# Inverse roots of the norms on GpSimd: a power and one Newton step instead of a square root and a reciprocal

## The chip, the cores and the metric

The kernel runs on one core of a Trainium2 chip. Five engines work side by side, each through its own queue and strictly in the order of that queue: TensorE (PE, with its weight loads PEld) for matrix products and transposes, VectorE (DVE), ScalarE (ACT) for functions that it reads from a loaded table, GpSimd (POOL), and SyncE (SP), which here only issues DMAs. They wait for each other through semaphores.

The metric is the time of one execution on the device in microseconds (us), as the median of several runs. Beside it stands one profiled execution, with its own time and a record of its instructions.

## The reference, cut to what matters

Input x has 8 sequences of 512 tokens with 256 features. There are two layers, and each has an attention-like part and an MLP-like part that both read the normalised x:

```python
def _layernorm(x, axis=-1, eps=1e-05):
    m = jnp.mean(x, axis=axis, keepdims=True)
    v = jnp.var(x, axis=axis, keepdims=True)
    return (x - m) / jnp.sqrt(v + eps)
...
xn = _layernorm(x)
x = x + attention(xn) + fp4_mlp(xn)      # layer 0
xn = _layernorm(x)
x = x + convolution(xn) + int4_linear(xn)  # layer 1
```

- The attention of layer 0 has 16 heads of 64 and 64 memory keys, mixes the heads before and after the softmax, and keeps for each row the 64 largest scores.
- The MLP of layer 0 quantises its inputs and its weights to FP4 in blocks of 16.
- The convolution of layer 1 is a gated input, a decaying recurrence along the sequence, and then a second norm over the features, `(y - mu) * rsqrt(var + 0.001)`, before a gated MLP and an output product.

So there are three norms for each sequence: of x (used by attention and by the MLP of layer 0), of the sum after layer 0, and inside the convolution. Each needs an inverse square root for each token, 512 in a sequence. They lie as a tile of 128 partitions by 4 columns.

## The kernel before, in words

**Stages.** A short start loads weights and transposes them (lines 745 to 844). Then comes attention over 8 batches (one sequence each), with 8 groups of rows for each batch (lines 1511 to 1718). A group computes scores on TensorE, evicts them with ScalarE (lines 1016 and 1052), finds the 64th largest value of each row by a search, and applies the result. The search counts values above a threshold on ScalarE (line 1082, Sign with an accumulated sum) or on VectorE (lines 1086 and 1088), and moves the threshold by a secant step (`narrow`, line 1100), which runs on GpSimd or on VectorE. On GpSimd the division in that step is a power with the exponent minus 1 (line 1134, `by<-gap,minus`). The new threshold is the tile `cur`. After the search VectorE picks the survivors (lines 1152, 1155 and 1179), and GpSimd builds the tile `mixd` for the second mixing of heads (line 1271).

A check of the results follows, with a branch that is skipped here. The second stage (from line 1769) holds the MLP of layer 0 for batches 1 to 7 and layer 1 for all batches. Batch 0's MLP and the quantised x of batch 1 are already made at the end of attention (`early_mlp`, line 1425, and `begin_last`, line 1498).

**What sets the order.** Nothing is issued in program order in the two big stages. `Plan` (line 113) collects operations with an engine, a cost and a due time, and `Plan.run` (line 146) simulates the engines and issues, among the operations whose inputs are ready, the one that is due first. In attention the costs are written at each `pl.add`, and the due times come from `DUE` (line 78). In the start and in the second stage `Straight` (line 197) gives the costs (line 232): a DVE operation on few columns 0.17, an ACT operation 0.22 plus 0.83 ns a column plus 1.3 for Sqrt, a POOL operation 0.35 plus 1.8 ns a column. The due time is there the length of the chain that follows (`tails`, line 131). An operation that moves to another engine, or gets another cost, can therefore change the order around it. In the second stage every instruction carries line 276, where `Straight` issues it, so its rows are told apart by the names of their tiles.

**The norms.** There are 32 of them, and each computes mean and variance on VectorE, the square root on ScalarE, the reciprocal on VectorE, and then scales.

- Start, for batch 0: lines 797 to 810, tiles `mv`, `sd` and `scr`.
- Attention, for batches 1 to 7, for `early_mlp` and for `begin_last`: `normed` (line 852) plans four operations, the load on SP (cost 4.0), `stats` on DVE (2.8), `root` on ACT (2.9) and `scale` on DVE (2.0). The tiles are `ln_mv`, `ln_sd`, `ln_ri`, and `scr`.
- Second stage, norm of x for batches 2 to 7 (`quantised`, line 1816) and first norm of layer 1 for all batches (`norm1`, line 1873): `layernorm` (line 347). It makes `ln_mr`, the product of mean and inverse root, on VectorE, and scales on ScalarE.
- Second stage, second norm of layer 1 (`norm2`, line 1892): the variance comes from TensorE in the tile `ps_tr`, `sd` and `ri` hold root and inverse, and TensorE spreads `ri` over the partitions (line 1917).

**POOL's other work.** In the second stage GpSimd does three products of each FP4 quantisation (`fp4_steps`, lines 379, 390 and 391; tiles `q_v` and `q_lo`), the residual sums (lines 1833 and 1837) and the sum with the bias (line 1931).

One more square root, in the first guesses of the search (line 583), is computed once.

Of the kernel before, what the change touches and what calls it, by code (L numbers as in the profile page):

```python
# [8 lines left out]
F32 = mybir.dt.float32  # L9
U32 = mybir.dt.uint32  # L10
AF = mybir.ActivationFunctionType
ALU = mybir.AluOpType
# [3 lines left out]
P = 128  # L16
B, N, D = 8, 512, 256
NT = N // P
# [302 lines left out]
def norm_stats(nc, pool, x):  # L321

    st = pool.tile([P, NT, 6], F32, name="ln_st")
    mv = pool.tile([P, NT, 2], F32, name="ln_mv")
    for t in range(NT):
        nc.vector.bn_stats(st[:, t, :], x[:, t, :])
        nc.vector.bn_aggr(mv[:, t, :], st[:, t, :])
    nc.vector.tensor_scalar(mv[:, :, 1], mv[:, :, 1], 1e-5, None, ALU.add)
    return mv


def norm_root(nc, pool, mv):
    sd = pool.tile([P, NT], F32, name="ln_sd")
    nc.scalar.activation(sd, mv[:, :, 1], AF.Sqrt)
    return sd


def norm_scale(nc, pool, x, xn, mv, sd):
    ri = pool.tile([P, NT], F32, name="ln_ri")
    nc.vector.reciprocal(ri, sd)  # L340
    for t in range(NT):
        nc.vector.tensor_scalar(
            xn[:, t, :], x[:, t, :], mv[:, t, 0:1], ri[:, t : t + 1], ALU.subtract, ALU.mult
        )


def layernorm(nc, pool, x, xn):

    mv = norm_stats(nc, pool, x)
    sd = norm_root(nc, pool, mv)  # L350
    ri = pool.tile([P, NT], F32, name="ln_ri")
    nc.vector.reciprocal(ri, sd)
    mr = pool.tile([P, NT], F32, name="ln_mr")
    nc.vector.scalar_tensor_tensor(mr, mv[:, :, 0], -1.0, ri, ALU.mult, ALU.mult)
    for t in range(NT):
        nc.scalar.activation(
            xn[:, t, :], x[:, t, :], AF.Identity, bias=mr[:, t : t + 1], scale=ri[:, t : t + 1]
        )
# [36 lines left out]
def fp4(nc, pool, src, parts, n, tag):  # L395

    q = {"src": src}
    for k, w in (("amax", n // BLK), ("scale", n // BLK), ("rec", n // BLK), ("v", n), ("a", n), ("lo", n), ("hi", n)):
        q[k] = pool.tile([P, w], F32, name=f"q_{k}_{tag}")[:parts]
    for _, _, step in fp4_steps(nc, q, parts, n):  # L400
        step()
    return q["lo"]
# [241 lines left out]
def block_kernel(ctx: ExitStack, tc: tile.TileContext, a: dict, out: bass.AP):  # L644
    nc = tc.nc
# [3 lines left out]
    const = ctx.enter_context(tc.tile_pool(name="const", bufs=1))  # L649
    ident = const.tile([P, P], F32, name="ident")  # L650
    make_identity(nc, ident)

    dram = ctx.enter_context(tc.tile_pool(name="dram", bufs=1, space=bass.MemoryType.DRAM))
    att = dram.tile([B * NT, P, D], F32, name="att")
# [42 lines left out]
    with ExitStack() as c0:  # L697
# [35 lines left out]
        small = c0.enter_context(tc.tile_pool(name="small", bufs=2))  # L733
        st = c0.enter_context(tc.tile_pool(name="st", bufs=6))
# [10 lines left out]
        with tc.tile_pool(name="prep", bufs=1) as prep, tc.tile_pool(name="prep_ps", bufs=1, space=PSUM) as pps:  # L745
            pl = Plan({})
            r = Straight(nc, pl, True)
# [13 lines left out]
            xn = scr.tile([P, NT * D], F32, name="scr").rearrange("p (t d) -> p t d", d=D)  # L761
# [37 lines left out]
            mv0 = prep.tile([P, NT, 2], F32, name="mv0")  # L799
            sd0 = prep.tile([P, NT], F32, name="sd0")  # L800
# [1 line left out]
                r.vector.bn_stats(st0[:, t, :], xn[:, t, :])  # L802
                r.vector.bn_aggr(mv0[:, t, :], st0[:, t, :])
            r.vector.tensor_scalar(mv0[:, :, 1], mv0[:, :, 1], 1e-5, None, ALU.add)
            r.scalar.activation(sd0, mv0[:, :, 1], AF.Sqrt)
            r.vector.reciprocal(sd0, sd0)
            for t in range(NT):
                r.vector.tensor_scalar(
                    xn[:, t, :], xn[:, t, :], mv0[:, t, 0:1], sd0[:, t : t + 1], ALU.subtract, ALU.mult
# [42 lines left out]
        def normed(pl, src, take, deps=()):  # L852

            o = {}

            def load():
                o["xn"] = scr.tile([P, NT * D], F32, name="scr").rearrange("p (t d) -> p t d", d=D)
                nc.sync.dma_start(o["xn"], src)

            def stats():  # L860
                o["mv"] = norm_stats(nc, small, o["xn"])

            def root():
                o["sd"] = norm_root(nc, small, o["mv"])

            def scale():
                norm_scale(nc, small, o["xn"], o["xn"], o["mv"], o["sd"])

            op = pl.add("SP", 4.0, load, deps, take)
            op = pl.add("DVE", 2.8, stats, [op])  # L870
            op = pl.add("ACT", 2.9, root, [op])
            return o, pl.add("DVE", 2.0, scale, [op])

        def tokens(pl, src):

            o, norm = normed(pl, src, ["scr", "xnT"])
            done = []
            for e in range(DC):
                def turn(e=e):
                    if e == 0:  # L880
                        o["xnT"] = x2p.tile([P, DC, N], F32, name="xnT")
                    o["pt"] = pt = ps_m.tile([P, 512], F32, name="ps_mi")
                    for t in range(NT):
                        nc.tensor.transpose(
                            pt[:, t * P : (t + 1) * P], o["xn"][:, t, e * P : (e + 1) * P], ident
                        )
                    o["pt", e] = pt

                def evict(e=e):
                    nc.scalar.copy(o["xnT"][:, e, :], o["pt", e])  # L890

                op = pl.add("PE", 0.5, turn, [norm], ["ps_m"], ["scr"] if e == DC - 1 else [])
                done.append(pl.add("ACT", 0.5, evict, [op], (), ["ps_m"]))
            return o, done
# [530 lines left out]
        def early_mlp(pl, b, ready):  # L1425

            o, norm = normed(pl, x_in[b], ["scr"], [ready])
            for t in range(NT):
                h, k = {}, {}
# [68 lines left out]
        def begin_last(pl, guard, ready):  # L1498
# [12 lines left out]
        pl = Plan(dict(  # L1511
            scr=1, xnT=2, ps_m=3, ps_s=2, ps_a=2, ps_y=1, v=1, q=2, k0=1, k1=1, raw=4, rp=2, at=2, y=1,
            xset=1, xqT=2, hset=1, hT=2,
        ), ("scr", "ps_m", "ps_s", "ps_a", "ps_y"))
# [16 lines left out]
        r = Straight(nc, pl)  # L1531
# [118 lines left out]
        for n, (b, g) in enumerate(groups):  # L1650
            if n % NG == 0:
                if b == 0:
                    o, xdone = o0, [pl.add("none", 0.0, lambda: None, (), ["xnT"])]
                else:
                    o, xdone = tokens(pl, x_in[b])
# [16 lines left out]
            w = {}  # L1672
# [59 lines left out]
        with tc.If(flag > 0):  # L1732
            nc.sync.dma_start(big[:, : 2 * n_qk], wqk_d)
            nc.sync.dma_start(kt[:, :, :MEM], mk_d.rearrange("p (c m) -> p c m", m=MEM))
            with tc.For_i(0, B) as b:
                pl = Plan()
                o, xdone = tokens(pl, x_in[bass.ds(b, 1)].rearrange("o p t d -> p (o t) d"))
# [3 lines left out]
                for n, g in enumerate(ORDERS[0]):  # L1741
# [16 lines left out]
                    w = {}  # L1758
# [14 lines left out]
    lp = Slots(ctx.enter_context(tc.tile_pool(name="lp", bufs=1)), 1)  # L1773
    sm = Slots(ctx.enter_context(tc.tile_pool(name="sm", bufs=1)), 2)
# [4 lines left out]
    pl = Plan({})  # L1779
    r = Straight(nc, pl)  # L1780
# [35 lines left out]
    def quantised(b):  # L1816

        x = bp.tile([P, NT, D], F32, name="xb")
        r.sync.dma_start(x, x_in[b])
        xn = qx.tile([P, NT, D], F32, name="xnb")  # L1820
        layernorm(r, sm, x, xn)
        xq = fp4(r, qx, xn.rearrange("p t d -> p (t d)"), P, NT * D, "x")
        xqT = transposed(xq.rearrange("p (t d) -> p t d", d=D), "xqT")
        return dict(b=b, xqT=xqT, x1=residual(b, x))
# [47 lines left out]

    def norm1(w):
        xn1 = lp.tile([P, NT, D], F32, name="xn1")
        layernorm(r, sm, w["x1"], xn1)
        w["xnT"] = transposed(xn1, "xn1T")

    def convolve(w):
# [13 lines left out]
    def norm2(w):  # L1892


        y = w["y"]
        pm = ps_l.tile([P, 512], F32, name="ps_l")
        for c in range(DC):
            r.tensor.matmul(pm, onesm, y[:, c, :], start=(c == 0), stop=(c == DC - 1))
        sq = lp.tile([P, DC, N], F32, name="sq")
        for c in range(DC):  # L1900
            r.vector.tensor_tensor(y[:, c, :], y[:, c, :], pm, ALU.subtract)
            r.scalar.activation(sq[:, c, :], y[:, c, :], AF.Square)

        pvar = ps_tr.tile([P, 512], F32, name="ps_tr")
        for t in range(NT):
            for c in range(DC):
                r.tensor.matmul(
                    pvar[:, t : t + 1], sq[:, c, t * P : (t + 1) * P], onesm[:, 0:1], start=(c == 0), stop=(c == DC - 1)
                )
        sd = lp.tile([P, NT], F32, name="sd")  # L1910
        r.vector.tensor_scalar(sd, pvar[:, :NT], 0.001, None, ALU.add)
        r.scalar.activation(sd, sd, AF.Sqrt)
        ri = lp.tile([P, NT], F32, name="ri")
        r.vector.reciprocal(ri, sd)
        pri = ps_l.tile([P, 512], F32, name="ps_l")
        for t in range(NT):
            r.tensor.matmul(
                pri[:, t * P : (t + 1) * P], ri[:, t : t + 1].to_broadcast([P, P]), ident, start=True, stop=True
            )
        for c in range(DC):  # L1920
            r.vector.tensor_tensor(y[:, c, :], y[:, c, :], pri, ALU.mult)
# [83 lines left out]
```

## Time and profile before

| | |
|---|---|
| median of 3 runs | 2432.99 us (2425.1 to 2435.9) |
| profiled execution, own time | 2431.61 us |
| its span, first to last instruction | 2429.9 us |
| PE busy | 2179.5 us (90%) |
| DVE busy | 2041.6 us (84%) |
| ACT busy | 1880.4 us (77%) |
| POOL busy | 1098.0 us (45%) |
| attention stage | about 60 to 1870 us |
| second stage | about 1870 to 2430 us |

How to read it: a row of the groups gives the source line, the engine, the operation, the tile written and the tiles read, the shape, the number of instructions, the busy time and the mean ns of one. Behind the second bar stands how long the engine sat idle before these instructions, and what ended most of that. `ACT_TABLE_LOAD` is ScalarE changing its table of functions. A row in order of time starts with the start and the duration in us; a bracket at its end says how long the engine had been idle and what released it. The chain that ended last is followed back from the last instruction, at each step to what released it. A stretch of time gives for each engine the busy time, and the granted TensorE clock.

### The profile page before, as it was taken

The numbers are of one execution on the slowest core, as the hardware profiler recorded it, in microseconds if no ns is written. First come the engines' busy times: TensorE is split into PE (matmuls) and PEld (weight loads), VectorE is DVE, ScalarE is ACT, GpSimd is POOL, SyncE is SP. The second block draws the span as 40 slices with busy tenths as digits, with TensorE's granted clock in tenths as the row PEclk, the third lists the DMA queues.
The fourth block names the chain that finished last, engine by engine and source line by source line (L and its number), as shares of the span: only waits on it lengthen the run. The fifth ranks groups of instructions, "written<-read, shape, count | busy, mean of one in ns | idle before, by whom it ended". The sixth has DMA issues, their size and how long they took to land. (4 is left out here: it accounts for less than half of the span.)

```text
span 2429.9 us, 57285 instructions
## 1 busy us (share of the span) xinstructions
PE 2179.5 (90%) x19593; PEld 1522.9 (63%) x19593; DVE 2041.6 (84%) x6443; ACT 1880.4 (77%) x5486; POOL 1098.0 (45%) x2677
## 2 busy tenths in 40 slices
PE   8789999999999999999999999999776889998987
PEld 7347766766776676577657657765555556666654
DVE  7898999978997998899789879979896898777672
ACT  4599999989989999898989899899953546543342
POOL 2424555435454553545445444545543554444230
PEclk9899999999999999999999999999888889999998
DMA  6642343243244224223422423343001210000000
GB/s 184 126 98 58 56 74 61 45 77 53 59 61 74 53 46 79 49 62 60 72 54 45 79 46 79 55 80 75 19 16 41 91 35 26 18 18 10 9 1 18
DMA packets 117139, 137.53 MB, mean 57 GB/s; under 512 B 20044, under 2 KB 102759, under 8 KB 116583
## 3 DMA queue, kind: packets, MB, share of 16 engines
q1 hardware_dynamic: 116838, 133.80, 27.2%
q8 instruction: 156, 2.56, 0.5%
q14 instruction: 145, 1.18, 0.2%
HBM read 27.32 MB, written 15.73 MB: 18 GB/s over the span
## 5 line engine op out<-in xcount | busy, mean ns | idle before, releaser
L1082 ACT ACTIVATE junk<-ring,cur 128x480 int8<-128x480 f32 (+40 forms) x1552 | 890.5, 590 | 42.9 <-POOL cur L1144 33.8
L1086 DVE TENSOR_SCALAR_CACHE_REDUCE junk<-ring,cur 128x520 int8<-128x520 f32 (+7 forms) x976 | 498.4, 542 | 79.5 <-POOL cur L1144 70.3
L1044 PE MATMUL ps_sc<-ring,blend 128*128 128x280 f32 (+48 forms) x1152 | 369.2, 439 | 58.6 <-ACT ring L1052 37.5
L1316 PE MATMUL ps_at<-mixd,ring 128*128 128x128 f32 x2560 | 352.2, 285 | 16.6 <-ACT at L1322 11.9
L1316 PEld LDWEIGHTS ps_at<-mixd,ring 128*128 128x128 f32 x2560 | 312.8, 193 | 64.2 <-issue 21.6
L1082 ACT ACTIVATION_READ_ACCUMULATOR junk<-ring,cur 128x1 f32 x1552 | 343.2, 221 | 0.0
L1152 DVE SCALAR_TENSOR_TENSOR y<-ring,cur 128x520 f32<-128x520 f32 (+56 forms) x512 | 301.3, 588 | 11.1
L1044 PEld LDWEIGHTS ps_sc<-ring,blend 128*128 128x128 f32 x1152 | 190.9, 193 | 188.8 <-ACT ring L1052 103.3
L1179 DVE SCALAR_TENSOR_TENSOR ring<-ring,kth 128x520 f32<-128x520 f32 (+56 forms) x512 | 278.5, 560 | 1.9
L1155 DVE MAX8 top<-y 128x8 f32<-128x520 f32 (+56 forms) x512 | 255.7, 499 | 17.6
L1016 ACT COPY raw<-ps_mi 128x284 f32<-128x284 f32 (+15 forms) x576 | 225.7, 439 | 41.7 <-DMA ring<-raw 33.6
L1052 ACT ACTIVATE ring<-ps_sc 128x272 f32<-128x272 f32 (+33 forms) x576 | 229.3, 430 | 36.4 <-PE ps_sc L1044 34.5
L1001 PE MATMUL ps_mi<-kt,qT 64*32 64x284 f32 (+15 forms) x4608 | 241.9, 440 | 9.1 <-ACT raw L1016 7.9
L1340 PEld LDWEIGHTS ps_y<-at,v 128*64 128x64 f32 (+1 forms) x6144 | 195.5, 138 | 79.8 <-ACT at L1322 36.6
L1340 PE MATMUL ps_y<-at,v 128*64 128x64 f32 (+1 forms) x6144 | 220.2, 225 | 17.2 <-ACT at L1322 12.9
L1134 POOL TENSOR_TENSOR by<-gap,minus 128x8 f32<-128x8 f32 x124 | 215.1, 1734 | 9.7
L1271 POOL TENSOR_TENSOR mixd<-mix,rden 128x256 f32<-128x256 f32 x256 | 168.3, 686 | 77.1 <-DVE rden L1260 55.3
L1098 POOL TENSOR_TENSOR cur<-base,raw 128x8 f32<-128x8 f32 x186 | 46.5, 250 | 343.0 <-ACT junk L1082 338.0
L1322 ACT COPY at<-ps_at 128x512 f32<-128x512 f32 x320 | 191.9, 603 | 7.8 <-PE ps_at L1316 7.8
L276 PE MATMUL ps_gu<-big,ring 128*128 128x352 f32 x448 | 148.8, 477 | 17.2 <-DVE hid L276 10.3
L1033 POOL MEMSET ring<- 128x56 f32 (+6 forms) x448 | 34.7, 124 | 251.4 <-DMA ring<-raw 247.3
L276 PE MATMUL ps_l<-ring,w 128*128 128x512 f32 x256 | 126.7, 641 | 20.2 <-DVE u L276 16.1
(304 smaller groups left out, 3894.7 us busy)
## 6 DMA issues: line engine op xcount, KB each, us to landing
ring<-raw SPq DMA_DIRECT2D x32, 288.0 KB
ring<-raw SPq DMA_DIRECT2D x32, 284.0 KB
ring<-raw SPq DMA_DIRECT2D x32, 256.0 KB
ring<-raw SPq DMA_DIRECT2D x32, 252.0 KB
ring<-raw SPq DMA_DIRECT2D x32, 224.0 KB
ring<-raw SPq DMA_DIRECT2D x32, 220.0 KB
ring<-raw SPq DMA_DIRECT2D x32, 192.0 KB
ring<-raw SPq DMA_DIRECT2D x32, 188.0 KB
```

The lines of the kernel that those rows point to most:

```text
L276: call = lambda: fn(*a, **k)
L1001: nc.tensor.matmul(some[u][j * SUB : (j + 1) * SUB, : n1 - n0], q["T"][rows, 4 * rnd + j, side, sub::2], kt[rows, 4 * rnd + j, n0:n1], sta ...
L1016: nc.scalar.copy(k["raw", 2 * rnd + u][:, n0:n1], k["of", rnd, n0][u][:, : n1 - n0])
L1044: nc.tensor.matmul(ps[:, : n1 - n0], blend.rearrange("p k i -> p (k i)"), s[:, b, n0:n1], start=True, stop=True,)
L1052: nc.scalar.activation(s[:, b, n0:n1], k["pb", b][i][:, : n1 - n0], AF.Copy if plain else AF.Exp, scale=DH ** -0.5)
L1082: nc.scalar.activation(junk, src, AF.Sign, bias=thr, scale=-1.0, accum_out=raw[:, b : b + 1])
L1086: nc.vector.tensor_scalar(junk, src, thr, 0.0, ALU.is_ge, ALU.add, accum_out=raw[:, b : b + 1])
L1152: nc.vector.scalar_tensor_tensor(y, src, cur[:, 0, b : b + 1], src, ALU.is_lt, ALU.mult)
L1155: nc.vector.max(out=top[:, b, 1:], in_=y)
L1179: nc.vector.scalar_tensor_tensor(src, src, kth[:, b : b + 1], e, ALU.is_ge, ALU.mult, accum_out=den[:, b : b + 1])
L1316: nc.tensor.matmul(pt[:n, b * P : (b + 1) * P], s[:, 4 * j + b, col : col + n], w["mix"][j][:, b, :], start=True, stop=True,)
L1340: nc.tensor.matmul(w["py"][j * DH : (j + 1) * DH, q * GR : (q + 1) * GR], vs[c][:n, k * DH : (k + 1) * DH], ats[c][:n, k, :], start=(c == ...
```

## The change

A new function computes the inverse root of `v` with five GpSimd instructions: a power with the exponent -0.5, which a constant tile `root` holds, and one Newton step, `ri * (1.5 - 0.5 * v * ri * ri)`. All 32 norms call it. The ScalarE square root and the VectorE reciprocal go out of all of them. In the attention stage the planned operation moves from ACT with the cost 2.9 to POOL with the cost 3.0. In the start and the second stage the planner sees five POOL operations of 0.36 each. The square root of the first guesses (line 583) stays as it is.

```diff
-def norm_root(nc, pool, mv):
-    sd = pool.tile([P, NT], F32, name="ln_sd")
-    nc.scalar.activation(sd, mv[:, :, 1], AF.Sqrt)
-    return sd
-
-
-def norm_scale(nc, pool, x, xn, mv, sd):
+def inverse_root(nc, ri, t, v, root):
+
+    nc.gpsimd.tensor_tensor(ri, v, root, ALU.pow)
+    nc.gpsimd.tensor_tensor(t, ri, ri, ALU.mult)
+    nc.gpsimd.tensor_tensor(t, t, v, ALU.mult)
+    nc.gpsimd.tensor_scalar(t, t, -0.5, 1.5, ALU.mult, ALU.add)
+    nc.gpsimd.tensor_tensor(ri, ri, t, ALU.mult)
+
+
+def norm_root(nc, pool, mv, root):
     ri = pool.tile([P, NT], F32, name="ln_ri")
-    nc.vector.reciprocal(ri, sd)
+    t = pool.tile([P, NT], F32, name="ln_t")
+    inverse_root(nc, ri, t, mv[:, :, 1], root)
+    return ri
...
-def layernorm(nc, pool, x, xn):
+def layernorm(nc, pool, x, xn, root):
 
     mv = norm_stats(nc, pool, x)
-    sd = norm_root(nc, pool, mv)
-    ri = pool.tile([P, NT], F32, name="ln_ri")
-    nc.vector.reciprocal(ri, sd)
+    ri = norm_root(nc, pool, mv, root)
...
+    root = const.tile([P, NT], F32, name="root")
+    nc.gpsimd.memset(root, -0.5)
...
-            r.scalar.activation(sd0, mv0[:, :, 1], AF.Sqrt)
-            r.vector.reciprocal(sd0, sd0)
+            sd1 = prep.tile([P, NT], F32, name="sd1")
+            inverse_root(r, sd0, sd1, mv0[:, :, 1], root)
...
-            op = pl.add("ACT", 2.9, root, [op])
+            op = pl.add("POOL", 3.0, root_, [op])
...
-        r.scalar.activation(sd, sd, AF.Sqrt)
         ri = lp.tile([P, NT], F32, name="ri")
-        r.vector.reciprocal(ri, sd)
+        st = lp.tile([P, NT], F32, name="st")
+        inverse_root(r, ri, st, sd, root)
```

## The prediction

> **What bounds the kernel now.** I read the busy time by stretch first, because an average over the whole span mixes three regimes. The columns are the stretch, its length, then busy us (and instructions) of PE, PEld, DVE, ACT, POOL, the granted clock, the DMA share and GB/s.
>
> ```profile
> 0.00:170.00 170.00, 136.82 (x1016) 87.19 (x1016) 142.63 (x446) 107.64 (x294) 49.88 (x215) 0.95 0.59 145
> 170.00:1700.00 1530.00, 1435.68 (x15654) 1020.60 (x15648) 1350.74 (x4859) 1419.67 (x4452) 749.94 (x2186) 0.99 0.34 62
> 1700.00:1870.00 170.00, 122.42 (x1123) 97.23 (x1123) 150.98 (x449) 108.61 (x321) 84.10 (x157) 0.86 0.05 15
> 1870.00:2376.00 506.00, 447.43 (x1707) 297.42 (x1706) 382.81 (x667) 231.71 (x402) 211.71 (x121) 0.94 0.09 30
> 2376.00:2430.00 54.00, 37.12 (x106) 20.51 (x104) 14.47 (x24) 12.81 (x19) 2.34 (x1) 0.83 0.04 14
> ```
>
> Attention (170 to 1700) is held by PE at 94% and ACT at 93%, with DVE at 88%; POOL has half of its time free. In the second stage (1870 to 2376) PE leads at 88%, DVE is at 76%, ACT at 46%, POOL at 42%. The last 54 us are one dependency chain.
>
> Next come the groups by line. The four rows that hold table loads (44, 9, 7 and 2) make 62, of 1283 ns each. Two of the rows, and those of the only power in the kernel and of its neighbours on POOL:
>
> ```profile
> L276 ACT ACT_TABLE_LOAD x44 | 56.5, 1283 | 10.9 <-PE ps_gu L276 9.4 <-PEq L1988 0.8
> L334 ACT ACT_TABLE_LOAD x9 | 11.5, 1283 | 0.2
> L1134 POOL TENSOR_TENSOR by<-gap,minus 128x8 f32<-128x8 f32 x124 | 215.1, 1734 | 9.7
> L1124 POOL TENSOR_SCALAR same<-same 128x8 f32<-128x8 f32 x124 | 42.4, 342 | 10.8
> L1137 POOL TENSOR_TENSOR by<-by,gap 128x8 f32<-128x8 f32 x124 | 29.0, 234 | 9.7
> ```
>
> **The change, part by part.** There are 32 norms: 1 at the start, 9 through the planned norm of attention (7 for the next batch's tokens, 2 at 1731 and 1813), and 22 in the second stage (6 of x, 8 first, 8 second norms).
>
> *Attention, ACT.* A norm there is this, in order of time:
>
> ```profile
> 1062.98 1.28 ACT L334 ACT_TABLE_LOAD   x1
> 1064.27 0.21 ACT L334 ACTIVATE ln_sd<-ln_mv 128x4 f32<-128x4 f32 x1
> 1064.49 1.28 ACT L1052 ACT_TABLE_LOAD   x1
> 1065.79 0.47 ACT L1052 ACTIVATE ring<-ps_sc 128x360 f32<-128x360 f32 x1
> ```
>
> The next useful work starts 2.81 us after the first load, so seven norms free 7 x 2.8 = 20 us of ACT: the upper bound of the gain. (The Trainium skill, "ScalarE: Activation LUTs", the section on table sets, prices an exp followed by a sqrt at two loads of about 2.7 us; by that it would be 39 us. The rows of 1283 ns decide.) But ACT shares the bound with PE, and PE has work queued while ACT reloads. In the 9 us around each of the five regular reloads (424, 637, 850, 1064, 1279) PE is busy 8.56, 8.47, 8.41, 8.54 and 8.41 us: idle 2.6 us in all five. At 177 PE waits 2.58 us for ACT's ring line 1052, and around 236 it is idle 0.9 us. The gain that PE can hand on is thus 2.6 + 2.6 + 0.9 = 6 us, the lower bound. I take 6: PE is the busier engine.
>
> *Attention, POOL.* Power, three multiplications and a multiply-add go into POOL's queue, among its search steps. The power over 8 columns takes 1.66 us uncontended, a plain 8-column operation 0.20. For 4 columns it lies between 0.93 (0.20 plus half of 1.46, if it goes by columns) and 1.66 (if it does not). I take 0.93: 1.46 us is far more than the fixed part that a plain operation shows. From the rows in order of time, starts on POOL are 0.28 us apart after a multiplication and 0.33 after a multiply-add. A root is 0.93 + 0.08 + 0.28 + 0.28 + 0.33 + 0.20 = 2.1 us alone. The means above exceed the uncontended values by 0.08 (power), 0.10 and some 0.04 each: with these it is 2.4 us (3.1 at the other end). Seven roots are 17 us on an engine with 780 us free. The batch's tokens are scaled at 1069 and not transposed before 1248, so the root itself can wait. What is queued behind it are search steps, whose users are DVE's and ACT's counts; that is cover only while these have other blocks to count. I charge nothing, up to 7 x 2.4 = 17 us if it is gone.
>
> *The port.* A rule speaks against the change: the Trainium skill, "SBUF — State Buffer", section on the two separate sides, says that a GpSimd instruction and a VectorE one with two SBUF inputs exclude each other for their whole length. By it, 32 powers of 0.93 to 1.66 us would block DVE for 30 to 53 us. The trace shows a power over which line 1179, with two SBUF inputs, runs on:
>
> ```profile
> 583.22 1.66 POOL L1134 TENSOR_TENSOR by<-gap,minus 128x8 f32<-128x8 f32 x1
> 583.24 0.77 DVE L1179 SCALAR_TENSOR_TENSOR ring<-ring,kth 128x536 f32<-128x536 f32 x1
> 584.27 0.78 DVE L1179 SCALAR_TENSOR_TENSOR ring<-ring,kth 128x544 f32<-128x544 f32 x1
> ```
>
> Both have their usual length, as at other powers; wide POOL operations do block (a 128x704 DVE step goes from 0.52 to 2.67 us beside a 128x1024 one). So I charge 0.
>
> *Start.* A load at 7.74 goes. The root of the first guesses stays on ACT; before, it found the sqrt table loaded, and now needs a load of its own at 35.6, in a chain that POOL later waits for (4.6 us at the first search). Cost 1.3 us, 0 if DVE is the later one. The first norm has its variance at 8.6 and gets its root at 10.7 instead of 9.5; PE is busy with weight transposes until 14. Zero, plus or minus 1.
>
> *Between the stages* the two roots finish at about 1732 and 1815, before DVE comes to their reciprocals (1733.5 and 1815.9): nothing.
>
> *Second stage, loads.* 41 loads lie there; one should stay. ACT is at 46%, so most cost nothing: PE's matmuls cover them. The chain that ended last holds four: at 2007.47, 2014.84 and two here.
>
> ```profile
> 2175.85 1.28 ACT L276
> ...
> 2177.37 1.28 ACT L276
> ```
>
> That is 4 x 1.28 = 5.1 us off; nothing if DVE and PE are as late without them.
>
> *Second stage, the norms.* From the end of the variance to the first scaled tile, the eight first norms take 3.89, 2.51, 3.07, 3.07, 3.43, 2.16, 2.16 and 0.68 us: 21.0. With a root of 2.4, and 0.35 for the product with the mean and the hops, 8 x 2.75 = 22.0: 1.0 more. The second norms take 1.93, 2.32, 1.94, 2.12, 1.81, 2.12, 2.12 and 0.46, in all 14.8, from the variance to the reciprocal; then 8 x 2.4 = 19.2. Half of them are on the chain: the last costs 2.4 - 0.46 = 1.9, half of the other 2.5 is 1.2, together 3.1. In the tail nothing covers a root:
>
> ```profile
> 2402.76 0.17 DVE sd L276
> ...
> 2402.96 0.21 ACT sd L276
> ...
> 2403.20 0.19 DVE ri L276
> ```
>
> Six norms of x are used late: nothing. Behind a root in POOL's queue stand the quantisation's products (1.8, 1.5, 1.4 us), and DVE's in-order queue stands behind the product with the mean. POOL's own pieces are some 4.4% of the chain (1% of the whole span, which is 24 us of 550). 22 x 2.4 = 53 us more at that share is 2.3 us. The DVE reciprocals saved (32 x 0.17) fill gaps.
>
> **The sum.** -6 + 1.3 - 5.1 + 1.0 + 3.1 + 2.3 = -3.4 us on the profiled execution, whose own time is 2431.61 (span 2429.9, 1.7 around it): 2428.2. The median shown is 2432.99, 1.4 above it; on that scale 2429.6. A difference of 0.5%, 12 us, is about what a measurement of this kernel can tell from no change.
>
> **Rivals.** *ACT is the true bound of attention.* From 1030 to 1110, around the reload at 1064, ACT is busy 79.8 of 80 us. If the 2.8 us come off each batch, attention gains 20 instead of 6, and the total is 2415.6. Against it: after 1110 DVE is the full engine, and PE has few gaps to fill.
>
> *The roots come late in the second stage, on the other side.* The order there is planned with 0.36 us for each POOL operation on 4 columns, 2.2 for a root with hops; the old root was planned at 1.5 on ACT and took 0.2 once its table was in, so its users found it early. If POOL's wide products push each of the 22 roots back by 1.2 us more, DVE stands at its head and the chain takes 22 x 1.2 = 26 us: 2456. It decides (beyond +12) from (12 + 3.4) / 22 = 0.7 us for each. For it: DVE's tiny variance steps average 678 ns there, held up by POOL. Against: POOL is idle 58% of that stage.
>
> *Search steps late.* DVE waits 70.3 us for cur from POOL in 24 waits, the longest 10.1. If each root lands before such a step, the 17 us above come on top: 2446.
>
> *The loads stay.* If a table change remains at the SiLUs or the signs, ACT keeps loads and POOL's work is added: some 2429.6 + 11 = 2441. Against it: every second-stage load stands at a root or brings the old set back; sign and absolute value run after SiLU's load without one.
>
> **How the numbers follow.** Sum as above: 0.45; ACT the bound: 0.24; late roots: 0.18; late search steps: 0.09; loads stay: 0.04. The sum's own range is 2421 to 2441. The first rival is the case of faster, with the low edge of the sum: 0.26. The slower cases are 0.31, of which the loads staying is partly within 12 us: 0.29. Same: 0.45. Leaving about one in ten out at each side, the range is 2411 to 2455.
>
> **What would show it.** Some 5 table loads instead of 62; no Sqrt but one; powers of 128x4 at about 0.9 us (1.7: the other end); in attention, ACT's busy time 20 us lower and the time to 1700 only some 6 shorter (20: the first rival); the tail from 2376 longer by 4 us; DVE's waits for ri or for cur. I am wrong if DVE waits for POOL's roots more than 15 us in total, or if the planned order changes so that other waits of PE move by more than these sums.

## The result, and the profile after

The changed kernel takes 2460.01 us (median of 6 runs, 2457.4 to 2464.83), beside 2433.88 us for the kernel before: a ratio of 1.0111 with a 95% interval of 1.0093 to 1.0129, 26.1 us slower. The forecast was 2429.6, in a range of 2411 to 2455. The profiled execution has 2459.39 us (span 2457.7).

The busy time by stretch of the changed kernel, with the columns of the forecast's first view. The stretches are moved to where the stages now end.

```profile
0.00:170.00 170.00, 138.26 (x991) 90.07 (x991) 140.40 (x427) 103.65 (x276) 50.30 (x213) 0.91 0.60 142
170.00:1700.00 1530.00, 1422.42 (x15487) 1012.02 (x15480) 1338.52 (x4805) 1398.96 (x4406) 746.64 (x2206) 0.99 0.36 61
1700.00:1893.00 193.00, 136.66 (x1328) 106.85 (x1324) 163.50 (x512) 120.05 (x360) 100.76 (x190) 0.85 0.12 23
1893.00:2400.00 507.00, 447.74 (x1696) 296.52 (x1695) 373.05 (x647) 181.58 (x345) 257.41 (x219) 0.94 0.09 29
2400.00:2458.00 58.00, 37.29 (x109) 20.58 (x107) 14.11 (x22) 8.55 (x14) 5.94 (x11) 0.80 0.05 17
```

ScalarE is busy 20.7 us less in 170 to 1700 (1398.96 against 1419.67), as the forecast said. Yet that stretch holds less work than before (PE has 15487 matmuls against 15654, 1422 us against 1436), which is a part of the 20.7, and attention is behind by 1700. It ends at 1893.2 instead of 1871.7 (the start of tile `bad`, the check of the results): 21.5 of the 27.8 us between the two profiles lie there. The second stage, from there to the last output DMA, is 560.3 us long, against 554.1. The DMA column of the second row is the one to notice: 0.36 where it was 0.34, and nobody had asked for more transfers.

The groups by line of the changed kernel that answer to the forecast's rows:

```profile
L276 ACT ACT_TABLE_LOAD x4 | 5.1, 1283 | 10.4 <-PE ps_gu L276 9.5 <-PEq L1996 0.8
L334 POOL TENSOR_TENSOR ln_ri<-ln_mv,root 128x4 f32<-128x4 f32 x9 | 10.6, 1176 | 9.3 <-DVE ln_mv L328 9.3
L1142 POOL TENSOR_TENSOR by<-gap,minus 128x8 f32<-128x8 f32 x124 | 212.3, 1712 | 9.7
```

With one more at line 1459 there are 5 table loads, where there were 62. The new power over 4 columns has a mean of 1.18 us in attention. How a root runs alone is seen in the tail, in order of time:

```profile
2429.14 0.16 DVE L276 TENSOR_SCALAR sd<-ps_tr 128x4 f32<-128x4 f32 x1 [2.70 <-PE ps_tr L276]
2429.38 1.01 POOL L276 TENSOR_TENSOR ri<-sd,root 128x4 f32<-128x4 f32 x1 [22.46 <-DVE sd L276]
2430.47 0.20 POOL L276 TENSOR_TENSOR st<-ri 128x4 f32<-128x4 f32 x1
...
2431.30 0.20 POOL L276 TENSOR_TENSOR ri<-ri,st 128x4 f32<-128x4 f32 x1
2431.56 1.22 PE L276 MATMUL ps_l<-ident,ri 128*128 128x128 f32 x4 [2.46 <-POOL ri L276]
```

The power takes 1.01 us, the root 2.12 from 2429.38 to 2431.50, against 0.93 and 2.1 in the forecast. So the instructions alone cost what was said, and the table loads are gone. The 26 us come from elsewhere.

### The profile page after: what moved, and what is told of

Same layout as the page of the kernel before. It is cut to its first block, busy times and chain, and to the rows that moved or that the text cites. A ratio compares the mean times of both kernels' runs of the same rounds, so it can differ in the third digit from the quotient of the medians.

```text
span 2457.7 us, 57351 instructions
## 1 busy us (share of the span) xinstructions
PE 2182.4 (89%) x19593; PEld 1526.0 (62%) x19593; DVE 2029.6 (83%) x6411; ACT 1812.8 (74%) x5397; POOL 1161.1 (47%) x2838
## 3 DMA queue, kind: packets, MB, share of 16 engines
q1 hardware_dynamic: 116838, 133.80, 28.5%
q14 instruction: 144, 1.18, 0.2%
## 5 line engine op out<-in xcount | busy, mean ns | idle before, releaser
L1090 ACT ACTIVATE junk<-ring,cur 128x312 int8<-128x312 f32 (+36 forms) x1552 | 886.5, 584 | 41.7 <-POOL cur L1152 27.9
L1094 DVE TENSOR_SCALAR_CACHE_REDUCE junk<-ring,cur 128x520 int8<-128x520 f32 (+7 forms) x976 | 502.2, 541 | 71.3 <-POOL cur L1152 69.6
L1052 PE MATMUL ps_sc<-ring,blend 128*128 128x280 f32 (+47 forms) x1152 | 370.1, 440 | 70.6 <-DMA ring<-raw 31.5
L1090 ACT ACTIVATION_READ_ACCUMULATOR junk<-ring,cur 128x1 f32 x1552 | 334.3, 215 | 0.0
L1009 PE MATMUL ps_mi<-kt,qT 64*32 64x284 f32 (+15 forms) x4608 | 233.5, 437 | 6.5 <-ACT raw L1024 3.3
L1348 PE MATMUL ps_y<-at,v 128*64 128x64 f32 (+1 forms) x6144 | 221.6, 225 | 19.0 <-ACT at L1330 14.9
L1330 ACT COPY at<-ps_at 128x512 f32<-128x512 f32 x320 | 192.2, 604 | 27.4 <-PE ps_at L1324 27.2
L975 PE MATMUL ps_mi<-xnT,big 128*128 128x128 f32 x1024 | 133.4, 285 | 6.7 <-ACT raw L1024 3.9
```

Source lines behind the costliest of these rows:

```text
L1009: nc.tensor.matmul(some[u][j * SUB : (j + 1) * SUB, : n1 - n0], q["T"][rows, 4 * rnd + j, side, sub::2], kt[rows, 4 * rnd + j, n0:n1], sta ...
L1052: nc.tensor.matmul(ps[:, : n1 - n0], blend.rearrange("p k i -> p (k i)"), s[:, b, n0:n1], start=True, stop=True,)
L1090: nc.scalar.activation(junk, src, AF.Sign, bias=thr, scale=-1.0, accum_out=raw[:, b : b + 1])
L1094: nc.vector.tensor_scalar(junk, src, thr, 0.0, ALU.is_ge, ALU.add, accum_out=raw[:, b : b + 1])
L1348: nc.tensor.matmul(w["py"][j * DH : (j + 1) * DH, q * GR : (q + 1) * GR], vs[c][:n, k * DH : (k + 1) * DH], ats[c][:n, k, :], start=(c == ...
```

## The experiments

Each run has its own runs of the kernel before on the same chip (medians 2434.8 to 2437.3); "+x" is the difference to those, the bracket the 95% interval of the ratio. One profiled execution stands up to 9.4 us beside the median of its kernel (`second_only`), so sizes are taken from the medians and a trace is used for where the time goes.

### One stage alone, and the order alone

The change does two things in attention: other instructions, and another engine and cost in the plan. The first four kernels separate them, and the stages.

`attn_only` has the change in attention alone, with its plan:

```diff
-            op = pl.add("ACT", 2.9, root, [op])
+            op = pl.add("POOL", 3.0, root_, [op])
```

(`root_` issues the five POOL instructions.)

> Only the nine norms of the attention stage are changed: five GpSimd instructions, planned on POOL at 3.0 as in the change; start and second stage as before. In the two profiles the attention stage ends 21.5 us later after the change (1871.7 to 1893.2), about 2 us of it from the start. If the loss belongs to this part alone: 2434 + 19 = 2453, and the second stage as long as before (554 us). If it came from the start and was only carried along: about 2434.

Measured: 2452.43, +15.3 (1.0070 [1.0044, 1.0097]).

`attn_old_order` issues the same POOL instructions from an operation still planned as `("ACT", 2.9)`, so every engine has the order of before:

```diff
-            op = pl.add("ACT", 2.9, root, [op])
+            op = pl.add("ACT", 2.9, root_, [op])
```

> The nine attention norms are computed by the five GpSimd instructions, but the planner is told what it was told before (ACT, 2.9), so every other instruction keeps its place in its queue. Theory A (the planned order is what costs): the instructions themselves are free and 20 us of ScalarE are freed, so 2434 - 6 to 2434 - 20, about 2424. Theory B (the roots hold up GpSimd's search steps): seven roots of 2.1 to 2.5 us, each passed on to the counts, 2434 + 15 = 2449 or more.

Measured: 2444.57, +7.5 (1.0034 [1.0022, 1.0045]).

`attn_new_order` keeps the square root and the reciprocal and has only the plan's line changed (`root` is still the square root on ScalarE):

```diff
-            op = pl.add("ACT", 2.9, root, [op])
+            op = pl.add("POOL", 3.0, root, [op])
```

> The nine attention norms keep ScalarE's square root and VectorE's reciprocal, but the planner is told what the change tells it (POOL, 3.0), so all queues have the order of the changed kernel. Theory A (order): as slow as the change in this part or slower, since the table loads are in it again: 2453 to 2470. Theory B (GpSimd's roots): no GpSimd roots are there, so about 2434, within 6.

Measured: 2470.91, +33.8 (1.0148 [1.0102, 1.0193]). With four runs this one is known least well, to 25 to 47 us.

`second_only` has the change in `layernorm` and `norm2` of the second stage, attention and start as before:

```diff
-    sd = norm_root(nc, pool, mv)
     ri = pool.tile([P, NT], F32, name="ln_ri")
-    nc.vector.reciprocal(ri, sd)
+    t = pool.tile([P, NT], F32, name="ln_t")
+    inverse_root(nc, ri, t, mv[:, :, 1], root)
...
```

> Only the 22 norms of the second stage are changed (their order is planned anew with them). In the two profiles the time from the end of attention to the last output is 554.1 us before and 560.3 after: 2434 + 6 = 2440. If the late roots of the second stage are the main cost, as the rival of the prediction has it: 2434 + 20 or more.

Measured: 2456.03, +18.9 (1.0078 [1.0050, 1.0106]).

What follows: the order costs, and much (33.8 with no new instruction). But the order is not all. The kernel with the old order is slower although its ScalarE is freed. And in the profile of `second_only` attention ends 11 us later (1883.0), though, but for the memset of the new constant, not one instruction or its order is different there. What these two share, and `attn_new_order` lacks, is the tile `root`.

### The place of the ring

The tile of 16 bytes stands behind `ident`, ahead of the weights' tile `big` and of `ring`, and takes 32 bytes. In the compiled program `ring` begins at byte 34560 of each partition before the change, which is 135 x 256; with the tile it begins at 34592. `shift_only` is the kernel before with only this:

```diff
     make_identity(nc, ident)
+    root = const.tile([P, NT], F32, name="root")
+    nc.gpsimd.memset(root, -0.5)
```

> The kernel before, with one thing added: the 16-byte tile of constants, and its one memset. Every root, every other instruction and the order of all of them are those of before; nothing is left out. The tile moves everything that lies behind it in SBUF by 32 bytes, so that the ring of scores no longer begins on a 256-byte line. In the profiles so far the packets of 1536 bytes took 137 ns in the two kernels without the tile and 159 ns in those with it, those of 1280 bytes 81 to 85 against 93 to 94, and the attention of two kernels that have the tile and hardly anything else in common ended 10 and 11 us later than before. Theory of the place: about 10 us slower than before (2447 against 2437), the slow packets in the profile, the end of attention near 1882 instead of 1872. Theory of the roots and the order: no difference, within 3 us of before, and the slow packets belong to something else.

Measured: 2451.75, +14.5 (1.0065 [1.0052, 1.0078]). A constant that nobody reads costs over half of the loss. The waits of 60 to 1720, first of the kernel before (waiting tile and line, releaser, us in total, times, longest):

```profile
POOL ring L1033 <- DMA ring<-raw: 247.3, 77, 12.6
ACT raw L1016 <- DMA ring<-raw: 33.6, 45, 2.0
PE ps_sc L1044 <- DMA ring<-raw: 16.1, 26, 1.7
```

and of `shift_only`:

```profile
POOL ring L1044 <- DMA ring<-raw: 264.8, 81, 12.5
ACT raw L1027 <- DMA ring<-raw: 37.5, 47, 2.0
PE ps_sc L1055 <- DMA ring<-raw: 23.9, 27, 2.4
```

The transfers `ring<-raw`, which spread each score group from ScalarE's copies into the ring, come later. PE waits 7.8 us more for them, ScalarE 3.9 more for a free copy. The packets of the queue take more of the 16 DMA engines' time, for the same number and the same 133.80 MB; first before, then `shift_only`:

```profile
q1 hardware_dynamic: 116838, 133.80, 27.2%
q1 hardware_dynamic: 116838, 133.80, 28.1%
```

The engines' own work on the ring is not slower: from 170 to 1700 an eviction into it on ScalarE takes 429 ns on average in `shift_only`, against 431 before, and VectorE's masking step (line 1179 before) 552 against 553.

The three kernels that follow are those of above (and the whole change) with the tile made 256 bytes wide, so that everything behind it moves by a whole line and `ring` is on one again:

```diff
-    root = const.tile([P, NT], F32, name="root")
+    root = const.tile([P, 64], F32, name="root")[:, :NT]
```

> The whole change, with the tile of constants made 256 bytes wide, of which the first 16 are used: all instructions and their order are those of the changed kernel, and the ring begins on a 256-byte line again, as before the change. Theory of the place: some 10 of the 26 us come back, about 2453 where the changed kernel would give 2463 beside this before of 2437; packets of 1536 bytes at 137 ns. Theory of the roots and the order alone: 2463, nothing comes back.

Measured: 2446.54, +9.3 (1.0042 [1.0029, 1.0055]); 16.8 of the 26.1 us come back.

> Only the roots of the attention stage by the power and the Newton step, in the order of issue of the kernel before, with the constants' tile 256 bytes wide. The roots of the start and of the second stage are as before. With the narrow tile this was 2444.6 beside 2437.1. Theory of the place: 10 us less, about 2434.5, that is 2 to 3 below before, and so the 6 us that the forecast gave to the freed ScalarE are then partly there. Theory of the roots and the order: as with the narrow tile, 2444.5.

Measured: 2431.10, −6.2 (0.9979 [0.9970, 0.9989]): faster than the kernel before, and 13.7 us better than with the narrow tile.

> Only the roots of the second stage (first norms and second norms) by the power and the Newton step, as the changed kernel issues them, with the constants' tile 256 bytes wide; attention as before. With the narrow tile this was 2456.0 beside 2437.1, in its profile attention +11 and the second stage +3.6. Theory of the place: about 10 us less, 2446, or +4 to +9 on before, all of it in the second stage. Theory of the roots and the order: 2456.

Measured: 2440.77, +3.5 (1.0021 [1.0008, 1.0035]); 15.4 us better.

`ring_off_line` asks which tile it is. Of the tiles that attention uses it moves `big` and `ring` alone (those of the second stage move with them, whose length stays: 557.9 us from `bad` to the end of the profile, 558.2 before):

```diff
+    const.tile([P, 8], F32, name="spacer")
     big = const.tile([P, DC * 2 * FI + FKC * D], F32, name="big")
...
         keep = c0.enter_context(tc.tile_pool(name="keep", bufs=1))
+        keep.tile([P, 56], F32, name="spacer2")
```

> The kernel before without any change of instruction or order; only an unused tile of 32 bytes stands ahead of the weights' tile and the ring, and one of 224 bytes behind them, so that these two begin 32 bytes past a 256-byte line and all tiles of the attention stage behind them (the chip's own copies of the scores among them, from which the transfers read) lie as before to within whole lines. If the place of the ring, which the transfers write, is the cause: 2448 to 2452, packets of 1536 bytes at 156 to 160 ns. If the place of the source or of the small tiles is: 2437, packets at 137 ns.

Measured: 2449.73, +14.9 (1.0059 [1.0037, 1.0081]). So it is these two. They were not moved one at a time, but only the ring is written by DMAs throughout attention.

`shift_64` moves by 64 bytes instead of 32 (`const.tile([P, 16], ...)`):

> The kernel before, its instructions and order, with the constants' tile and its memset added as in the run with the 16-byte tile, but 64 bytes wide, so that weights' tile and ring begin 64 bytes past a 256-byte line where they were 32 past. If a transfer pays for every start that is not on a line of 256: as with 32, about 2450, packets of 1536 bytes at 156 to 160 ns. If only the half of a 64-byte line costs: 2437 and 137 ns.

Measured: 2450.81, +15.2 (1.0066 [1.0044, 1.0089]).

The mean time of a packet by its size, from the DMA records of each trace, fits this. Beside it stands the number of 256-byte lines that a packet touches when it starts 0, 32 or 64 bytes past one (each row of a group starts a multiple of 256 bytes into the ring):

| bytes | lines at 0 / 32 / 64 | before, ns | 32 past (`shift_only`) | 64 past (`shift_64`) |
|---|---|---|---|---|
| 1248 | 5 / 5 / 6 | 78.7 | 79.3 | 95.4 |
| 1280 | 5 / 6 / 6 | 80.6 | 95.6 | 99.8 |
| 1504 | 6 / 6 / 7 | 126.4 | 125.3 | 143.8 |
| 1536 | 6 / 7 / 7 | 136.8 | 156.2 | 162.3 |
| 2016 | 8 / 8 / 9 | 194.9 | 195.2 | 215.7 |
| 2048 | 8 / 9 / 9 | 245.0 | 256.9 | 256.6 |

At these sizes a packet gets slower when it touches one line more. Sizes that are whole lines suffer at once; those that end 32 bytes short of a line bear a shift of 32 but not of 64. Not every size is as clean: 1792 bytes show 179.9, 194.4 and 185.3, 2304 show 249.9, 260.9 and 249.7, and 1760 rise in two steps, 174.9, 183.2 and 192.2. (Between traces that differ in neither the ring's place nor attention's order a size varies by up to 7 ns.) Short packets hardly mind: 512 bytes take 30.1, 30.3 and 31.9 ns, 768 take 36.6, 36.8 and 37.7, although both touch a line more.

The Trainium skill has a rule of this form, in "DMA: Bandwidth & Descriptors", the section on how a descriptor splits into AXI transactions: a transaction must begin on a 256-byte boundary, so a transfer that starts elsewhere begins with one from the boundary below, whose first bytes are not used. If time went by the number of transactions, 1536 bytes 32 past a line would take 7 in place of 6, by estimate 17% more, and the rows show 14%; but 512 bytes would take 3 in place of 2, 50% more, and the rows show 1%. So the count tells which of the longer sizes slow down, and not by how much. The page speaks of bytes fetched; here it is the place written to.

`raw_on_line` tries the place read from. The copies `raw` start 64 bytes past a line in the kernel before; here an unused tile ahead of their pool puts them on one, in the kernel of `attn_old_whole_lines`:

```diff
+        qp_.tile([P, 48], F32, name="spacer", bufs=1)
         o0 = {}
```

> The best kernel so far (attention's roots on POOL in the old order, ring on its line: 2431 beside 2437), with an unused tile of 192 bytes that puts the score copies, from which the transfers read, on a 256-byte line as well; they begin 64 past one in all kernels so far. If the read side pays as the write side does: 3 to 10 us less, 2421 to 2428. If the write side alone pays: 2431, packets as before.

Measured: 2431.98, −3.6 (0.9984 [0.9970, 0.9998]): no gain over −6.2, and packets of 1536 bytes take 141.2 ns instead of 136.9. Reading from 64 bytes past a line shows no price.

### The order in attention

With the place set right, the order can be priced. `attn_only_whole_lines` is `attn_only` with the wide tile:

> Only the roots of the attention stage by the power and the Newton step, planned on POOL as the change plans them (3.0 on POOL in place of 2.9 on ScalarE), with the constants' tile 256 bytes wide. It differs from the kernel with the same roots in the old order (2431.1 beside 2437.3) by the order of issue alone. Theory of the order: the new plan costs 10 to 14 us against the old one, so about 2443 here, 6 above before. Theory that the place did all of it: as in the old order, 2431.

Measured: 2439.91, +5.1 (1.0014 [1.0005, 1.0024]). Against the same instructions in the old order (−6.2) the plan of the change costs 11.3 us. (The two profiles are 16 us apart, since the second stands 7.8 above its median.) Where it goes, in the waits of 60 to 1720, first with the old order (`attn_old_whole_lines`):

```profile
DVE junk L1102 <- POOL cur L1160: 72.9, 27, 10.2
DVE o L1384 <- PE ps_mi L1380: 36.0, 9, 11.6
PE ps_sc L1060 <- DMA ring<-raw: 17.3, 26, 1.6
```

then with the order of the change (`attn_only_whole_lines`):

```profile
DVE o L1384 <- PE ps_mi L1380: 67.2, 13, 11.7
DVE junk L1102 <- POOL cur L1160: 65.8, 27, 6.9
PE ps_sc L1060 <- DMA ring<-raw: 29.9, 28, 2.5
```

VectorE's waits for the search on POOL are not longer. What grew are waits for transfers that are issued at other moments, 12.6 us more on PE, and VectorE's before `o`, the eviction of the output product. The POOL roots don't make them, for `attn_new_order`, which has the new order without them, waits as long:

```profile
DVE o L1368 <- PE ps_mi L1364: 68.6, 14, 10.9
PE ps_sc L1044 <- DMA ring<-raw: 29.5, 26, 2.5
```

 Another piece lies at the end of attention, where `early_mlp` quantises the last tokens. PE in order of time, first the old order:

```profile
1837.52 1.54 PE L1487 MATMUL ps_sc<-ident,kt 128*128 128x128 f32 x6 [6.57 <-POOL kt L400]
```

then that of the change:

```profile
1845.37 0.69 PE L1426 MATMUL ps_mi<-ident,xnT 128*128 128x128 f32 x2 [6.51 <-POOL xnT L400]
1855.54 1.54 PE L1487 MATMUL ps_sc<-ident,kt 128*128 128x128 f32 x6 [9.49 <-POOL kt L400]
```

From the start of the last copy of scores to the end of attention it is 163 to 165 us in the eleven traces with attention's old order, with or without the change's instructions, and 168 to 170 in the five with the change's order. So about 5 of the 11 us lie in that end. From 1800 on PE waits 28.1 us for POOL's quantisation products (`xnT`, `kt`), against 14.3 in the old order.

Is POOL as the planned engine to blame, or the cost of 3.0? Two kernels of the same instructions and places change nothing but the planner's figure. `plan_act_short`:

```diff
-            op = pl.add("ACT", 2.9, root_, [op])
+            op = pl.add("ACT", 1.0, root_, [op])
```

> The attention stage's roots by the power and the Newton step on POOL, the constants' tile 256 bytes wide, all else as before: the instructions of the kernel that gave 2431. Only the planner's figure for the root is changed, 1.0 on ScalarE's line where it was 2.9. That alone reorders about as much of every engine as the plan of the change does (434 lines of PE's order differ, against 499). If the price of the changed plan is that its roots stand on POOL's line: as the old order, 2429 to 2433. If any new order costs, because the old one was the best of many: 2436 to 2446.

Measured: 2446.55, +10.9 (1.0050 [1.0031, 1.0069]), at the edge of the second case.

`plan_pool_short`, with the figure that the trace gives for a root:

```diff
-            op = pl.add("POOL", 3.0, root_, [op])
+            op = pl.add("POOL", 2.0, root_, [op])
```

> The same instructions and places once more, the root planned on POOL as in the change, but at 2.0, about what the trace measures for one (2.1), in place of 3.0. If the figure of 3.0 or POOL's line is what costs: nearer the old order for the first, 2431 to 2435, or the same as the changed plan for the second, 2438 to 2442. If each order is a draw: anywhere between 2431 and 2446.

Measured: 2454.38, +18.8 (1.0084 [1.0061, 1.0108]), slower than any case foresaw.

Neither explains it: the order costs with the root on ScalarE's line too, and more with the lower figure on POOL's. Each change of the plan, the more truthful figure too, rearranges the engines, and the three new orders, that of the change first, cost 11.3, 17.1 and 25.0 us against the old one. In attention the due times are written by hand (`DUE`), and the order that they give with the figures of before is the best of the four. Freeing ScalarE of the loads is worth 6.2 us in that order; in the order of the change it is worth 33.8 − 5.1 = 28.7 (19 to 46 by the ends of the two intervals), as much as the 20 us of its seven reloads or more. A gain has no size of its own without an order. Why these orders come out worse than the old one, beyond the waits shown, and whether there is a better one, stays open.

One rival was not tested: the granted TensorE clock. It is lower where the time is longer, on average over the runs 0.9631 before, 0.9643 in `attn_old_whole_lines`, 0.9612 in `attn_only_whole_lines` and 0.9572 in the changed kernel, and within each kernel's own runs the time rises by about 1.5 us for each 0.001 less. By that estimate some 9 us of the changed kernel's 26, and 5 of the 11.3 that the order costs, come together with a lower clock. Whether the clock makes the time or the waits lower the clock, no run shows. The ring's price does not need it: `shift_64` has 0.9630 and is 15.2 us slower.

### The second stage

`second_old_whole_lines` has the roots of the second stage on POOL, wide tile, in the order of before. The planner is told of the old square root and reciprocal, and the five instructions are issued in their place:

```diff
-    nc.scalar.activation(sd, mv[:, :, 1], AF.Sqrt)
-    nc.vector.reciprocal(ri, sd)
+    nc.scalar.activation(ri, mv[:, :, 1], AF.Sqrt,
+        issue=lambda *_: inverse_root(nc.nc, ri, half, mv[:, :, 1], root))
+    nc.vector.reciprocal(ri, ri, issue=lambda *_: None)
```

> The roots of the second stage by the power and the Newton step on POOL, issued where the plan of the kernel before has its square root and with its order on every engine, constants' tile 256 bytes wide; attention as before. With the order that the change plans it was 2440.8 beside 2437.3. If the late roots behind POOL's wide fp4 products make the 3.5 us: 2440 to 2446 here, since the old order does not know of POOL. If the new order of the second stage makes them: the freed table loads are left, 2432 to 2436.

Measured: 2458.29, +23.5 (1.0090 [1.0065, 1.0115]), above both cases. In the profile, which stands 6.8 us above the median, the second stage is 24.6 us longer than before (582.8 from `bad` to the end, against 558.2); attention, with nothing changed in it, ends 8.9 us later there.

`all_old_whole_lines` adds the roots of attention in the old order:

> Both stages' roots on POOL, both in the order of the kernel before, constants' tile 256 bytes wide; the start's root as before. The sum of the single steps: 2431 from attention, and what the second stage in the old order shows. If that gains, 2426 to 2430; if its roots come late, 2434 to 2440. This is the forecast's own case, the change of instructions without a change of order or place, for which it said 2433.9 less 3.4.

Measured: 2458.20, +23.4 (1.0086 [1.0063, 1.0110]), with a second stage of 583.1 us in the profile. The 6.2 us of attention do not show beside the run before; the interval of 15 to 27 us still holds the 17.3 of the sum.

So here the change of order helps: +3.5 with the order that the change plans, +23.5 without it. (The new order with the old square roots was not run, so how much of the 20 us it would give by itself is not known.) In the waits from 1870 on, `second_old_whole_lines` has these for a root:

```profile
DVE ln_mr L276 <- POOL ln_ri L338: 9.8, 10, 2.5
PE ps_l L276 <- POOL ri L338: 5.2, 3, 2.5
```

and the changed kernel these:

```profile
PE ps_l L276 <- POOL ri L276: 7.0, 2, 4.5
DVE ln_mr L276 <- POOL ln_ri L276: 4.1, 6, 2.2
```

The direct waits are small. In the old order the time from the variance to the inverse root, over the eight second norms, sums to 22.4 us against 14.8 before, and the time from the variance to `ln_mr`, over the 14 norms of x and first norms, to 67.8 against 53.8: 21.5 us for 22 roots, 1.0 us each. That is about the 23.5 measured, which fits a delay that is handed on whole; it was not tested root by root. In the changed kernel these times are longer still, 34.1 and 104.4, or 3.2 us more for each root than before, since the planner, which knows of POOL, sets the roots between the products:

```profile
2240.73 1.59 POOL L276 TENSOR_TENSOR ri<-sd,root 128x4 f32<-128x4 f32 x1 [7.52 <-DVE sd L276]
2242.39 0.20 POOL L276 TENSOR_TENSOR st<-ri 128x4 f32<-128x4 f32 x1
2242.67 0.20 POOL L276 TENSOR_TENSOR st<-st,sd 128x4 f32<-128x4 f32 x1
2242.83 1.70 POOL L276 TENSOR_TENSOR q_lo_h<-q_lo_h,q_v_h 128x704 f32<-128x704 f32 x1
2244.49 0.19 POOL L276 TENSOR_SCALAR st<-st 128x4 f32<-128x4 f32 x1
2244.65 1.38 POOL L276 TENSOR_TENSOR q_lo_h<-q_lo_h,q_scale_h 128x704 f32<-128x704 f32 x1
2245.99 0.20 POOL L276 TENSOR_TENSOR ri<-ri,st 128x4 f32<-128x4 f32 x1
```

Two quantisation products of the MLP run inside this root, which so takes 5.46 us, and its users lose little: PE had other matmuls ahead of `ps_l`, and waited 1.39 us for the product `q_lo_h`; VectorE then stood idle 1.80 us for `ps_l`. So a late root is cheap where the order has other work ahead of its users. The power here takes 1.59 us instead of 1.01, beside VectorE's steps; the eight powers of second norms average 1.30.

## Why the prediction was wrong

| step of the sum | forecast | measured | by |
|---|---|---|---|
| attention's roots, order and place kept | −6 | −6.2 | `attn_old_whole_lines` |
| the order planned for attention | no term | +11.3 | 5.1 − (−6.2) |
| second stage, with its own order (−5.1 + 1.0 + 3.1 + 2.3) | +1.3 | +3.5 | `second_whole_lines` |
| start | +1.3 | +0.7, the remainder, not run alone | 9.3 − 5.1 − 3.5 |
| the tile of constants | no term | +16.8 | 26.1 − 9.3 |
| sum | −3.4 | +26.1 | |

The measured terms sum to the total because the start is what remains; any effect of the parts on each other is in it.

*Attention, ACT.* Right that PE hands on only a part of ScalarE's 20 us, in the order of before: −6.2 with the ring on its line, and 7.5 − 14.5 = −7.0 with the ring off it. That the number 6 is met is in part luck. It rests on 2.6 us of PE idle in 45 us around five reloads, but PE is idle for 94.3 of the 1530 us of that stretch, on average 2.8 in 45 us, so there is no excess beside the reloads; and of the 0.9 us around 236, 0.37 were a wait for POOL. The rival by which ScalarE is the true bound, at 20 us, is ruled out for the old order and not for that of the change.

*Attention, POOL, and the rival of late search steps.* Right to charge nothing: VectorE waits 69.6 us for `cur` in the changed kernel, 70.3 before. The port, also charged at nothing, was not tried by itself; the −6.2 leave it no visible price in attention.

*Loads.* Right: 5 are left. That the loads stay is ruled out.

*Second stage.* The forecast took late roots as a rival, 1.2 us for each and +26. With the order of before it is nearly so: 1.0 us each, +23.5. In the changed kernel the roots are later than that, 3.2 us each, and the stage still costs only 3.5. So the forecast's own step, a few us for half of the norms on the chain, is near for the kernel as it is, but not for the reason given: the roots do come late, and the planned order has room for them. With order and place both kept, the forecast's sum would have failed here instead: the same instructions in `all_old_whole_lines` cost +23.4, not a few us less. Of the two conditions named for being wrong, the first did not occur (VectorE waits 4.1 us for POOL's roots).

*What failed first: "The change, part by part" had no term for the tile of constants.* It counted the instructions of the change and left out that `root = const.tile(...)` stands ahead of the ring. This is the largest term, +16.8 in the changed kernel, +14.5 when done alone, and 10 to 17 us in the five pairs of kernels with the ring off its line and on it. The tile stood in the diff, and that the ring is what DMAs write in attention stood in the profile's rows; the two were not put together.

*What failed second: the sum took attention's order as kept.* The other condition, "if the planned order changes so that other waits of PE move by more than these sums", is what happened, at +11.3 us. The text had it as a condition and gave it no price and no chance. Nothing in the sum said what another order than the one set by hand would cost.

The version that follows from this, attention's roots on POOL in the old order with the ring on its line and the second stage left on ScalarE, is the fastest of the study at 0.9979 [0.9970, 0.9989] of the kernel before: 6 us.

## What to carry to other kernels

Before you add a tile, however small, ask what lies behind it and whether DMAs write there; here padding it to a whole 256-byte line took the price away (10 to 17 us). Where a planner sets the order, price the change of order as a step of its own, and separate it by issuing the new instructions from the old plan's slots. The sign is not given: for the second stage's roots the new order was worth 20 us (+3.5 against +23.5), for attention's it cost 11.3.

## What the runs showed of the hardware that was not expected

- In these SBUF-to-SBUF transfers most packets of 1248 bytes and more slow down when the place they write to touches one 256-byte line more: 1536 bytes take 136.8 ns on a line and 156.2 with a start 32 past it; 1504 bytes take 126.4, 125.3 and, 64 past, 143.8. Packets of 512 and 768 bytes show 1% or less at 32 past. For this kernel it is 14.5 to 15.2 us of 2435. The side read from showed no such price (136.9 ns from 64 past a line, 141.2 from the line).
- A power on POOL takes 1.66 us over 8 columns and 1.01 over 4 when undisturbed. If time goes in a line with the columns, that is by estimate 0.16 us each and some 0.36 us beside them (1.01 − 4 x 0.1625). A plain multiplication takes 0.20 us over either.
